# A sparse graph-attention kernel: score products with 32 weight columns per head instead of two

## The chip, the core and the metric

One NeuronCore of a Trainium2 chip runs the whole program. Its engines work side by side and wait for each other through semaphores: TensorE (matmuls, PE in the profile, with its weight loads shown as PEld), VectorE (DVE), ScalarE (ACT), GpSimd (POOL) and SyncE (SP, which here only starts DMAs). The metric is device time in microseconds of one execution. Five runs of the kernel before took 3256.15 to 3273.82 us, with a median of 3261.12 us.

## What is computed

Two graph layers over 3327 nodes with 128 features and a sparse weighted adjacency matrix. The first layer is a four-head GATv2 attention. Cut to what matters here:

```python
h = relu(layernorm(x))
for each head:
    x1, x2 = h @ w1, h @ w2
    E = leaky_relu(x1[:, None, :] + x2[None, :, :], 0.01)
    s = E @ a                          # one score for each pair of nodes
    s = exp(8 * tanh(s / 8)) * adj
    s = s / sum(s, axis=-1)
    out = leaky_relu(s @ h @ Wlin.T, 0.01)
x = x + concat(heads) @ w
```

The second layer is a graph convolution with the same matrix, relu(A_norm @ (relu(layernorm(x)) @ W.T + b)), added to x. The change touches the line `s = E @ a` of the first layer.

## The kernel before

Nodes are padded to 3328 and handled in 26 blocks of 128 rows, each in two halves of 64 rows. Only neighbours are computed: for each half, four windows of up to 8 x 128 pairs (row, neighbour) and a fifth, smaller window for what didn't fit. DVE finds the neighbours (`prep`, lines 353 to 570), POOL fetches the neighbours' rows by indirect DMA into tiles `g` (`gather`, L595), and a fixed sequence written out in `_sparse_layers` works the windows off. The order on each engine is the order in which this Python code issues instructions; `slot()` advances the older windows' tails (`finish`, `close`), the next block's preparation, and the fetches by one step each time that it is called.

A window is worked in groups. For windows 0 to 3 a group is half a window, 512 pairs; for the fifth window it is 320 pairs. `stage_z` transposes the neighbours' features on TensorE, head by head, into the PSUM tile `z` (L622; L625 and L627 for the fifth window), and DVE takes the maximum with the row's own negated features and writes `r` (L638; L633 with L635 on ACT for the fifth). With slope 0.01 the leaky part is a multiple of the plain sum, which comes from precomputed products, so that what is left of the score is one product of `r` with the vector `a` times 0.99.

`stage_r` is that product. For each of the four heads `h` it multiplies the weights `sel[:, h, ...]` with the 512 columns of `r` and writes to partitions 32h and 32h+1 of the PSUM tile `s`. `sel` holds, for each head, the vector in column 31 and zeros around it (L1139, L1140). In the kernel before it is 33 columns wide: with `at` = 0 the two columns taken are 31 and 32, with `at` = 1 they are 30 and 31, so the first half of a window lands in row 32h and the second, added to it, in row 32h+1. The rest of `s` is set to zero once (L650) and never written. The products of a window's two halves are issued together, after the second one's `r` (`k.held`): eight products in a row for windows 0 to 3 and four for the fifth, 36 for each half block.

`finish` then takes the window on: ACT copies `s` to SBUF (`ssb`, L666), TensorE transposes it (L675), DVE adds the precomputed parts to give `sc` (L678, L681), ACT computes `th` = tanh (L686) and `pe` = exp (L688), DVE multiplies with the adjacency weights into `wt` (L697), and TensorE sums the neighbours' features (L706: four column groups of 32 columns; L724 for the fifth window). `sc` and `th` come from a pool with two buffers each, so one window's may be written while the last one's is still read. A tile with one buffer has to be read out before its next writing.

When L706 is done, the window's `g` tile is free and POOL may issue the next fetch into it.

SBUF is close to full: four `g` tiles of 22,784 bytes per partition lie at the end of it.

Of the kernel before, what the change touches and what calls it, by code (L numbers as in the profile page):

```python
# [9 lines left out]
F32 = mybir.dt.float32  # L10
# [5 lines left out]
P = 128  # L16
# [215 lines left out]
def _sparse_layers(tc, nc, x, adj, w1, w2, a, wlin, w, gw, gb, gb_sb, gwT, x_sb, dinv, flag, ident, out):  # L232
# [14 lines left out]
    H = w1.shape[0]  # L247
# [5 lines left out]
    WT = 8  # L253
# [3 lines left out]
    with ExitStack() as l0:  # L257
        res = l0.enter_context(tc.tile_pool(name="res", bufs=1))
# [9 lines left out]
        w1_sb = res.tile([P, H, D], F32, name="w1_sb")  # L268
        wlinT = res.tile([P, H, D], F32, name="wlinT")
        w_sb = res.tile([P, H, D], F32, name="w_sb")  # L270
        sel = res.tile([P, H, 33], F32, name="sel")
        p_all = res.tile([P, NB, 2 * H], F32, name="p_all")
        code = res.tile([P, NP], mybir.dt.uint16, name="code")
        epos = res.tile([P, 2 * FOUND], F32, name="epos")
# [11 lines left out]
        pb = l0.enter_context(tc.tile_pool(name="pb", bufs=2))  # L286
# [358 lines left out]
        def stage_r(k, hb, m, rs):  # L645
            n = 4 * P if m < 8 else FOUND * P + HALF
            at = m % 2
            if state["scores"] is None:
                state["scores"] = ps_s.tile([P, BANK], F32, name="s")
                nc.vector.memset(state["scores"], 0.0)  # L650
            k.s = state["scores"]
            if at == 0 and m < 8:
                k.held = rs
                return
            for at, r in ((0, k.held), (1, rs)) if at else ((0, rs),):
                for h in range(H):
                    nc.tensor.matmul(k.s[32 * h:32 * h + 2, :n], sel[:, h, 31 - at:33 - at], r[h // 2][:, h % 2, :n],  # L657
                                     start=(at == 0), stop=(at == 1 or m == 8))


        def finish(k, hb, w):
            g, s = k.g.pop((hb, w)), k.s
            f0 = k.f0[hb]
            nt, nk, nm = (WT, 4, 2) if w < NW else (OVT, OVT, 1)
            ssb = ph.tile([P, BANK], F32, name="ssb", bufs=1)
            nc.scalar.copy(ssb[:, :nk * P], s[:, :nk * P])  # L666
            if w < NW:
                wq = pb.tile([P, WT, 8], F32, name="wq")
                diag = bass.AP(g.tensor, g.offset + BODY * hb, [list(g.ap[0]), [WIDE + 8, 8], [1, 8]])
                nc.vector.tensor_tensor(wq, diag, qmask[:, None, :].to_broadcast([P, WT, 8]), OP.mult)  # L670
            yield
            yield
            pt = ps_tr.tile([P, 4, P], F32, name="tr")
            for q in range(nk):
                nc.tensor.transpose(pt[:, q, :], ssb[:, q * P:(q + 1) * P], ident)  # L675
            yield
            sc = pb.tile([P, WT, H], F32, name="sc")
            nc.vector.tensor_tensor(sc[:, :nt].rearrange("p (m k) h -> p m k h", m=nm),  # L678
                                    pt.rearrange("p k (h m) -> p m k h", m=32)[:, :nm, :nk],
                                    g[:, :, f0 + D:f0 + D + H].rearrange("p (m k) h -> p m k h", m=nm), OP.add)  # L680
            nc.vector.tensor_add(sc[:, :nt], sc[:, :nt], k.pex[:, 8 * hb:8 * hb + 8] if w < NW else  # L681
                                 k.ex[:, OVT * hb:OVT * hb + OVT, 42:42 + H])
            yield
            yield
            th = pb.tile([P, WT, H], F32, name="th")
            nc.scalar.activation(th[:, :nt], sc[:, :nt], AF.Tanh, scale=1.0 / CAP)  # L686
            pe = pb.tile([P, WT, H], F32, name="pe")
            nc.scalar.activation(pe[:, :nt], th[:, :nt], AF.Exp, scale=CAP)  # L688
            yield
            yield  # L690

            if w == 0:
                k.ag = ps_a.tile([P, 2, 256], F32, name="ag")
            ag = k.ag
            if w < NW:
                wt = pv.tile([P, WT, H, 8], F32, name="wt", bufs=2)
                nc.vector.tensor_tensor(wt, pe[:, :, :, None].to_broadcast([P, WT, H, 8]),  # L697
                                        wq[:, :, None, :].to_broadcast([P, WT, H, 8]), OP.mult)
                yield
                yield  # L700
                yield
                yield
                yield
                for t in range(WT):
                    u, cg = t // 4, t % 4
                    nc.tensor.matmul(ag[32 * cg:32 * cg + 32, u, :WORK], wt[:, t].rearrange("p h q -> p (h q)"),  # L706
                                     g[:, t, f0:f0 + WORK], start=(w == 0 and t < 4), stop=False, skip_group_check=True)
                allow("g")
                return
            am = pb.tile([P, OVT, HALF], F32, name="am", bufs=1)  # L710
            wo = pv.tile([P, OVT, 8, H, 8], F32, name="wo")
            for t in range(OVT):
                nc.vector.scalar_tensor_tensor(am[:, t, :], code[:, :HALF], k.ex[:, OVT * hb + t, 41:42], g[:, t, BODY * hb:BODY * hb + HALF],
                                               op0=OP.is_equal, op1=OP.mult)
                nc.vector.tensor_tensor(wo[:, t], pe[:, t, None, :, None].to_broadcast([P, 8, H, 8]),
                                        am[:, t].rearrange("p (g q) -> p g q", q=8)[:, :, None, :].to_broadcast([P, 8, H, 8]), OP.mult)
                yield
            yield
            yield
            yield  # L720
            yield
            for t in range(OVT):
                for u in range(2):
                    nc.tensor.matmul(ag[:, u, :WORK], wo[:, t, 4 * u:4 * u + 4].rearrange("p g h q -> p (g h q)"),  # L724
                                     g[:, t, f0:f0 + WORK], start=False, stop=(t == OVT - 1), skip_group_check=True)
            allow("ge")
            tails.append(close(k, hb))
# [75 lines left out]
        for b in range(NB):  # L803
            k = Blk()
# [40 lines left out]
        def allow(kind):  # L845
            state[kind] += 1
# [345 lines left out]
        with tc.manual_schedule():  # L1192
# [4 lines left out]
            n = len(groups)  # L1197
            def scores(i):
                if 0 <= i < n:
                    b, hb, m = groups[i]  # L1200
                    stage_r(blks[b], hb, m, rs.pop(i))
                    if m % 2 or m == NG - 1:
                        ends.append(finish(blks[b], hb, m // 2))
                    slot()
# [81 lines left out]
def kernel(  # L1286
# [26 lines left out]
    gb_sb = const.tile([P, D], F32, name="gb_sb")  # L1313

    _sparse_layers(tc, nc, x, adj, w1, w2, a, wlin, w, gw, gb, gb_sb, gwT, x_sb, dinv, flag, ident, out)


# [46 lines left out]
```

## Time and profile before

| | |
|---|---|
| Median of five runs | 3261.12 us |
| Profiled execution | 3291.75 us, span 3290.0 us |
| Mean granted TensorE clock | 0.898 |
| DVE r L638, maxima | 1013.5 us busy, 832 instructions, mean 1218 ns |
| PE z L622, transposes of windows 0 to 3 | 1048.9 us busy, 6656 instructions, mean 300 ns |
| POOL g L595, indirect DMAs | 1593.1 us busy, 1664 instructions |
| ACT ssb L666, copies of s | 147.0 us busy, 260 instructions, mean 565 ns |
| ACT th L686 | 58.5 us busy, 260 instructions, mean 225 ns |
| DMA, mean over the span | 251 GB/s |

How to read it: busy time is the time in which at least one instruction of the group was running, the mean is that of one instruction, and matmuls overlap, so that count times mean is more than busy. PE rows are matmuls and PEld rows the loads of their weights. A matmul of four-byte floats is recorded as two matmuls and two loads; a transpose as one of each. In a row such as "128*2 128x512", 128*2 is rows times columns of the weights and 128x512 is the moving data. The chain of waits is followed back from the last instruction and tells where time sets the end; idle time of an engine that isn't on it costs nothing. The granted clock is the share of TensorE's clock pulses that the throttle let through.

### The profile page before, as it was taken

The page shows a single profiled execution, that of the slowest core. Times are in us where ns is not written, and L with a number is a line of the kernel's source. Part 1 is how long each engine was busy: PE and PEld are TensorE (multiplying, and loading weights), DVE is VectorE, ACT ScalarE, POOL GpSimd, SP SyncE. Part 2 cuts the span into 40 slices and gives each one's busy share as a digit, 9 for nine tenths or more (in the row PEclk, how much of TensorE's full clock was granted, in tenths as well). Part 3 has the DMA queues.
Part 4 walks back from the last instruction along what each step waited for, and adds up shares of the span by engine and source line. Part 5 has one row for each costly group of instructions (what it writes and reads, how often), then busy time and mean ns, then how long its engine had stood idle before and what let it go on. Part 6 is the DMA issues. An engine that isn't in the chain of part 4 may idle for free.

```text
span 3290.0 us, 52385 instructions
## 1 busy us (share of the span) xinstructions
PE 2564.1 (78%) x19410; PEld 1796.3 (55%) x19410; DVE 2102.2 (64%) x6426; ACT 682.1 (21%) x1703; POOL 1718.0 (52%) x1822
## 2 busy tenths in 40 slices
PE   6688777877788787778777787777877787777887
PEld 4455555555565565565555555555555555555553
DVE  6577676767667666666666665665666666665442
ACT  3122122212212221221221221221221221221110
POOL 3555555555555555545545555555555455555520
PEclk8789898998988989889989898998988999997999
DMA  9978788778877877867867867877777777777886
GB/s 320 339 263 262 242 263 276 228 260 269 265 234 257 278 215 253 275 204 261 275 211 247 266 218 242 260 246 225 260 241 230 251 256 238 245 232 224 266 265 191
DMA packets 417844, 826.94 MB, mean 251 GB/s; under 512 B 38435, under 2 KB 288815, under 8 KB 414255
## 3 DMA queue, kind: packets, MB, share of 16 engines
q0 software_dynamic: 141440, 619.41, 57.3%
q1 hardware_dynamic: 165343, 147.87, 14.5%
q10 hardware_dynamic: 110800, 56.25, 5.8%
q8 instruction: 156, 2.56, 0.3%
q14 instruction: 105, 0.86, 0.1%
HBM read 754.47 MB, written 113.22 MB: 264 GB/s over the span
## 4 chain that ended last, share of the span: by engine, by line
PE 55%; DVE 16%; issue 11%; another core or an unknown queue 9%; DMA 5%; POOL 2%; ACT 1%; SPq 0%; ACTq 0%; DVEq 0%; POOLq 0%
PE z L622 20%; PE s L657 12%; DVE r L638 9%; PE ag L706 4%; PE z L627 3%; PE tr L675 3%; DVE cand L422 2%; POOL g L595 2%; PE ag L724 2%; DMA g<-table,idx 2%; PE tr L379 2%; DVE codes L410 1%; PE tr L757 1%; PE tr L365 1%
## 5 line engine op out<-in xcount | busy, mean ns | idle before, releaser
L595 POOL DMA_INDIRECT g<-table,idx x1664 | 1593.1, 957 | 1278.7 <-PE ag L706 651.5
L638 DVE TENSOR_TENSOR r<-z,x1n 128x1024 f32<-128x1024 f32 x832 | 1013.5, 1218 | 736.2 <-remote 307.8
L622 PE MATMUL z<-ident,g 128*128 128x128 f32 x6656 | 1048.9, 300 | 216.0 <-issue 140.3
L622 PEld LDWEIGHTS z<-ident,g 128*128 128x128 f32 x6656 | 845.5, 155 | 412.0 <-issue 271.3
L657 PE MATMUL s<-r,sel 128*2 128x512 f32 (+1 forms) x3744 | 527.5, 613 | 71.7 <-issue 55.9
L666 ACT COPY ssb<-s 128x512 f32<-128x512 f32 x260 | 147.0, 565 | 854.0 <-remote 265.3
L706 PE MATMUL ag<-g,wt 128*32 128x133 f32 x3328 | 206.7, 295 | 76.7 <-issue 75.8
L657 PEld LDWEIGHTS s<-r,sel 128*2 128x2 f32 x3744 | 82.3, 85 | 336.9 <-issue 301.5
L706 PEld LDWEIGHTS ag<-g,wt 128*32 128x32 f32 x3328 | 125.1, 114 | 185.6 <-issue 176.1
L422 DVE MAX8 cand<-codes 128x8 f32<-128x52 uint16 x1664 | 217.3, 205 | 0.0
L379 PE MATMUL tr<-at,x_sb 128*128 128x128 f32 x488 | 97.5, 356 | 128.3 <-ACT at L367 102.9
L675 PE MATMUL tr<-ident,ssb 128*128 128x128 f32 x988 | 165.6, 291 | 37.2 <-ACT ssb L666 18.6
L367 ACT COPY at<-tr 128x512 f32<-128x512 f32 (+1 forms) x175 | 97.3, 556 | 393.8 <-remote 188.5
L595 POOL DMA_INDIRECT ge<-table,idxo x104 | 101.2, 973 | 145.0 <-PE ag L724 70.8
L379 PEld LDWEIGHTS tr<-at,x_sb 128*128 128x128 f32 x488 | 81.9, 251 | 153.8 <-ACT at L367 116.6
L686 ACT ACTIVATE th<-sc 128x32 f32<-128x32 f32 x260 | 58.5, 225 | 506.9 <-DVE sc L681 234.7
L675 PEld LDWEIGHTS tr<-ident,ssb 128*128 128x128 f32 x988 | 123.9, 149 | 58.8 <-ACT ssb L666 28.0
L633 DVE TENSOR_TENSOR r<-z,x1n 128x128 f32<-128x128 f32 x104 | 30.1, 290 | 185.9 <-PE z L627 120.0
L627 PE MATMUL z<-oi,x1b 128*128 128x256 f32 x416 | 131.5, 395 | 13.3 <-issue 13.2
L365 PE MATMUL tr<-ident,adjb 128*128 128x128 f32 x676 | 121.3, 307 | 25.6 <-DMA adjb<-in_adj_dram 15.5
L453 DVE MAX8 lists<-cand 128x8 f32<-128x272 f32 (+1 forms) x338 | 133.2, 394 | 2.2
L622 PE MATMUL z<-ident,ge 128*128 128x128 f32 x416 | 87.1, 285 | 42.6 <-issue 35.9
(199 smaller groups left out, 2583.8 us busy)
## 6 DMA issues: line engine op xcount, KB each, us to landing
adjb<-in_adj_dram SPq DMA_DIRECT2D x26, 1664.0 KB
table<-AT_d SPq DMA_DIRECT2D x26, 1664.0 KB
AT_d<-at ACTq DMA_DIRECT2D x150, 256.0 KB
g<-table,idx POOLq DMA_INDIRECT x1664
table<-img SPq DMA_DIRECT2D x12, 1296.0 KB
adjb<-AT_d SPq DMA_DIRECT2D x72, 128.0 KB
g<-AT_d SPq DMA_DIRECT2D x25, 256.0 KB
g<-AT_d ACTq DMA_DIRECT2D x25, 256.0 KB
```

Source lines behind the costliest of these rows:

```text
L365: nc.tensor.transpose(pt[:, q, :], adjb[:, (j0 + q) * P:(j0 + q + 1) * P], ident)
L379: nc.tensor.matmul(pq[:, :P], x_sb[:, j0 + q, :], at[:, q, :], start=(q == 0), stop=(q == js[-1]))
L422: nc.vector.max(cand[:, c, 8:].rearrange("p (r s) -> p r s", s=32)[:, :, sgm % 32], codes.rearrange("p a b -> p (a b)")[:, sgm % 32 * SEG: ...
L453: nc.vector.max(top, of)
L595: return nc.gpsimd.indirect_dma_start(out=g[:, t, lo:hi], out_offset=None, in_=tab, in_offset=bass.IndirectOffsetOnAxis(ap=at[:, t:t + 1], ...
L622: nc.tensor.matmul(z[:, i, q * P:(q + 1) * P], g[:, m % 2 * 4 + q, c0:c0 + D], ident, is_transpose=True, start=(q == 0 or m < 8), stop=(m ...
L627: nc.tensor.matmul(z[:, i, :n], k.x1b[:, h * D:(h + 1) * D], k.oi[:, hb * n:(hb + 1) * n], start=False, stop=True, skip_group_check=True)
L638: nc.vector.tensor_tensor(r.rearrange("p h (i s) -> p h i s", s=16), z.rearrange("p h (i s) -> p h i s", s=16), k.x1n[:, 2 * hp:2 * hp + 2 ...
L657: nc.tensor.matmul(k.s[32 * h:32 * h + 2, :n], sel[:, h, 31 - at:33 - at], r[h // 2][:, h % 2, :n], start=(at == 0), stop=(at == 1 or m == 8))
L666: nc.scalar.copy(ssb[:, :nk * P], s[:, :nk * P])
L675: nc.tensor.transpose(pt[:, q, :], ssb[:, q * P:(q + 1) * P], ident)
L706: nc.tensor.matmul(ag[32 * cg:32 * cg + 32, u, :WORK], wt[:, t].rearrange("p h q -> p (h q)"), g[:, t, f0:f0 + WORK], start=(w == 0 and t ...
```

## The change

`sel` becomes 63 columns wide, with the vector still in column 31. Each product takes 32 columns of it instead of two: 31 to 62 with `at` = 0 and 30 to 61 with `at` = 1. It writes all 32 partitions of its head, 30 of them with zeros (or zeros added). The number, order and moving data of the products stay. `sel` grows by 4 x 30 x 4 = 480 bytes per partition; `sc` and `th` get one buffer instead of two, which gives back 128 bytes each.

```diff
@@ -268,7 +268,7 @@
-        sel = res.tile([P, H, 33], F32, name="sel")
+        sel = res.tile([P, H, 63], F32, name="sel")
@@ -654,7 +654,7 @@
                 for h in range(H):
-                    nc.tensor.matmul(k.s[32 * h:32 * h + 2, :n], sel[:, h, 31 - at:33 - at], r[h // 2][:, h % 2, :n],
+                    nc.tensor.matmul(k.s[32 * h:32 * h + 32, :n], sel[:, h, 31 - at:63 - at], r[h // 2][:, h % 2, :n],
                                      start=(at == 0), stop=(at == 1 or m == 8))
@@ -674,7 +674,7 @@
-            sc = pb.tile([P, WT, H], F32, name="sc")
+            sc = pb.tile([P, WT, H], F32, name="sc", bufs=1)
@@ -682,7 +682,7 @@
-            th = pb.tile([P, WT, H], F32, name="th")
+            th = pb.tile([P, WT, H], F32, name="th", bufs=1)
```

## The prediction

> **What bounds the kernel now.** I read the page first: busy shares, the granted clock, the chain that ended last, and the groups of the two lines that matter here.
>
> ```profile
> PE 2564.1 (78%) x19410; PEld 1796.3 (55%) x19410; DVE 2102.2 (64%) x6426; ACT 682.1 (21%) x1703; POOL 1718.0 (52%) x1822
> PEclk8789898998988989889989898998988999997999
> ...
> PE 55%; DVE 16%; issue 11%; another core or an unknown queue 9%; DMA 5%; POOL 2%; ACT 1%; SPq 0%; ACTq 0%; DVEq 0%; POOLq 0%
> PE z L622 20%; PE s L657 12%; DVE r L638 9%; PE ag L706 4%; PE z L627 3%; PE tr L675 3%; DVE cand L422 2%; POOL g L595 2%; PE ag L724 2%; DMA g<-table,idx 2%; PE tr L379 2%; DVE codes L410 1%; PE tr L757 1%; PE tr L365 1%
> ...
> L657 PE MATMUL s<-r,sel 128*2 128x512 f32 (+1 forms) x3744 | 527.5, 613 | 71.7 <-issue 55.9
> ...
> L706 PE MATMUL ag<-g,wt 128*32 128x133 f32 x3328 | 206.7, 295 | 76.7 <-issue 75.8
> L657 PEld LDWEIGHTS s<-r,sel 128*2 128x2 f32 x3744 | 82.3, 85 | 336.9 <-issue 301.5
> L706 PEld LDWEIGHTS ag<-g,wt 128*32 128x32 f32 x3328 | 125.1, 114 | 185.6 <-issue 176.1
> ```
>
> TensorE is busiest and holds 55% of the chain; the rest is short waits shared among all engines. The score products L657 are 12% of the chain, 395 us of their 527.5 us busy, so three quarters of their time sets the end. L706 is this kernel's own example of the new form: four column groups of 32 columns at full depth, four-byte floats.
>
> Then I took both lines apart by source line (columns: count, then ns minimum/median/maximum).
>
> ```profile
> L657 PEld LDWEIGHTS s<-r,sel x3744: 80/83/129, 98.7 to 3194.7; 128*2 128x2 f32 x198
> L657 PE MATMUL s<-r,sel x3744: 431/592/1061, 98.7 to 3195.2; 128*2 128x512 f32 x176, 128*2 128x320 f32 x22
> ...
> L706 PEld LDWEIGHTS ag<-g,wt x3328: 106/110/178, 117.8 to 3205.6; 128*32 128x32 f32 x196
> L706 PE MATMUL ag<-g,wt x3328: 273/277/431, 118.3 to 3205.7; 128*32 128x133 f32 x196
> ```
>
> And a stretch of the timeline in order (start us, length us, then engine, line, count).
>
> ```profile
> 1528.84 0.11 PEld L657 LDWEIGHTS s<-r,sel 128*2 128x2 f32 x8
> ...
> 1529.27 0.10 PEld L657 LDWEIGHTS s<-r,sel 128*2 128x2 f32 x4 [0.33 <-issue]
> 1529.70 0.10 PEld L657 LDWEIGHTS s<-r,sel 128*2 128x2 f32 x4 [0.33 <-issue]
> ...
> 1530.13 0.13 PEld L706 LDWEIGHTS ag<-g,wt 128*32 128x32 f32 x4 [0.33 <-issue]
> ...
> 1530.56 0.64 PE L706 MATMUL ag<-g,wt 128*32 128x133 f32 x16
> ```
>
> Each product is recorded twice, so 26 blocks x 2 halves x 36 products are the 3744 records. The four heads run at once already: a four of loads every 0.43 us, at 1529.27, 1529.70 and 1530.13, each for the four of matmuls that follows. The last four is L706's, with 32 columns, and its matmuls start 0.43 us later too: a four of 32-column loads was hidden behind a four of streaming.
>
> **The change, part by part.** The order of instructions on every engine stays as it was; only the width of L657 and some waits differ. So nothing moves past a queue.
>
> *Streaming.* Does a 32-column product take longer than a 2-column one? L657 gives 592 ns for 512 moving columns and 431 ns for 320, so 161/192 = 0.84 ns per column. Carried down to 133 columns that is 274 ns; L706, with 32 weight columns, has 273 minimum, 277 median. The weight columns cost at most 3 ns of latency, under 2 us over 468 groups of products (26 x 2 x 9). Cost: 0.
>
> *Weight loads.* 80/83 ns becomes 106/110 ns, so 27 ns more per four (the four loads start a few ns apart and overlap). There are 3744/4 = 936 fours. If every one is covered: 0. If none is: 936 x 29 ns (the difference of the means, 114 - 85) = 27 us. In between: counting records, 1412 loads start within 4 ns of a matmul of their line, so about 353 fours stand at the head of a burst with nothing to hide behind: 353 x 27 ns = 9.5 us, of which the three quarters on the chain are 7 us. I take 7, since the timeline shows the others hidden; 0 and 27 stay as the bounds.
>
> [...] The timeline shows L657's loads at 1529.27 beside a stream that runs to 1529.70. [...]
>
> *The clock.* The granted clock is either full or half here, in steps of 3.41 us, and averages 0.898: (1 - 0.898) x 2 x 3290 = 671 us at half. If wider weights counted as more activity, this edit would buy speed. Stretches of 3.41 us (busy us and count for PE, PEld, DVE, ACT, POOL, then granted clock, DMA share, GB/s):
>
> ```profile
> 943.83:947.24 3.41, 1.30 (x7) 0.14 (x5) 2.21 (x6) 0.00 (x0) 1.90 (x2) 1.00 0.88 286
> 947.24:950.65 3.41, 3.41 (x29) 2.74 (x27) 2.54 (x11) 0.99 (x2) 1.01 (x2) 0.50 0.34 114
> ...
> 2305.74:2309.16 3.42, 1.94 (x17) 0.31 (x16) 0.44 (x4) 0.24 (x1) 2.39 (x3) 1.00 1.01 335
> 2309.16:2312.57 3.41, 3.01 (x27) 3.01 (x28) 2.23 (x10) 1.52 (x3) 0.00 (x0) 1.00 0.82 282
> ```
>
> The same stretch for L657 alone:
>
> ```profile
> 2305.74:2309.16 3.42, 1.90 (x16) 0.31 (x16) 1.00 1.01 335
> ```
>
> A stretch with 1.30 us busy is followed by half clock; one with 1.94 us, nearly all 2-column products, by full. I put this through all 762 stretches at full clock, with streaming time taken from the spacings (0.43 us per four of 512; a run of eight transposes takes 1.04 us, its last 0.27, so 0.11 us each): a streaming share under 0.37 is followed by half clock and one over it by full, with one exception. 74 stretches are over it only if the 2-column products count in full, and all 74 kept the clock. So width doesn't count. Cost: 0.
>
> *Single buffers for sc and th.* L678 must now wait until the tanh L686 has read the last sc. Among the 259 pairs in the trace the tightest is this one, from ACT's and DVE's timelines:
>
> ```profile
> 3196.44 0.23 ACT L686 ACTIVATE th<-sc 128x32 f32<-128x32 f32 x1
> 3196.70 0.23 ACT L688 ACTIVATE pe<-th 128x32 f32<-128x32 f32 x1
> ...
> 3198.65 0.17 DVE L678 TENSOR_TENSOR sc<-tr,ge 128x12 f32<-128x12 f32 x1 [8.10 <-PE tr L675]
> ```
>
> 1.97 us from the tanh's end to the next sc; the second tightest is 3.74 us. th is written and read on ACT in order, 2.12 us apart at least. Were ACT 2 us late, L678 would hold up DVE, with the maxima L638 of the next group behind it, and TensorE behind those. The built program has 162 more semaphore instructions on ACT and 8 on DVE; such records take 17 ns on ACT (median), so 2.8 us on an engine that is 79% idle. Bounds 0 and 3 us; I take 0, as ACT's own lateness is the cover.
>
> *Memory.* sel's memset grows by 120 elements once, in the start. Every tile behind sel lies 480 bytes further on, those behind sc and th 224. The maxima L422 read 32 slices 104 bytes apart, and their medians by slice are 202 to 215 ns in no order of address; gather packets of 5224 and 5248 bytes, from halves with different row starts, share a minimum of 201 ns. Nearest bounds: none to 1% of those 217 us, 2 us either way. I take 0.
>
> **Sum.** 3291.75 us is the profiled execution (span 3290.0, 1.75 around it); plus 7 is 3298.75, or +0.21%. That execution is 0.94% above the median 3261.12 and above all five runs, so I carry over the ratio: 3261.12 x 1.0021 = 3268 us.
>
> **The rivals.** (a) *Slower: the loads are paid everywhere.* Place: PEld ahead of L657. [...] Against it: L706's four fours take 0.64 us in the timeline, so they start (0.64 - 0.28)/3 = 0.12 us apart, with loads of 110 ns between. Price 27 us on 3291.75, 0.82%: 3288 us. It passes 0.5% (16.5 us) when over 570 of the 936 fours pay. (b) *Faster: width counts for the clock.* Of the 127 stretches after which the clock fell, 20 hold any score products. TensorE streams 0.75 of the half-clock time, so that time costs 671 x 0.75 / 2 = 252 us, 2.0 per fall; 20 saved are 40 us, times TensorE's 55% of the chain 22 us: 3291.75 - 22 gives 3239 us. Against it: the 74 stretches. (c) *The single buffers hold up DVE.* Each of 260 windows would have to lose 1.97 us of slack first; 3 us otherwise, 3264 us with no load term. (d) *Timing or addresses shift the falls of the clock by chance.* At 2.0 us a fall, 8 falls more or fewer are 16 us: either sign, 3245 to 3277 us. The five runs span 0.54%, so it does happen.
>
> **How the numbers follow.** Within 0.5% is about what a measurement of this kernel can tell from no change. The forecast, with (c) at 3 us in it, 0.58. (a) 0.20; (b) 0.12; (d) or a longer wait beyond 0.5%, 0.05 each way. So faster 0.12 + 0.05 = 0.17, same 0.58, slower 0.25. The range reaches from (b) to (a): 3240 to 3290. The likeliest case's own range, load term from 0 to 16 us with the runs' spread of about 8 us either way, is 3253 to 3285.
>
> **What would show it.** Loads at L657 of 106 to 110 ns; its 512-column products still 592 ns and 0.43 us apart by fours; mean clock within 0.01 of 0.898; no wait of L678 on ACT beyond the few now. I am wrong if the fours are further apart than 0.43 us at full clock, if stretches with little but L657 change which clock follows them, or if L638, L595 or a DMA changes its time per instruction, which would point to addresses.

## The result, and the profile after

The changed kernel takes 1.0021 times the kernel before, with a 95% interval of 1.001 to 1.0032 (52 runs with a median of 3281.0 us against 94 with 3274.86): 6.9 us more, 3 to 10. The forecast was +0.21% and no change by the bound of 0.5%. The number was met; what follows shows that two of the parts that it was added up from were not.

The page after, with the lines that answer to those before:

```profile
span 3298.4 us, 52555 instructions
PE 2584.2 (78%) x19410; PEld 1831.2 (56%) x19410; DVE 2100.7 (64%) x6426; ACT 683.4 (21%) x1703; POOL 1709.6 (52%) x1822
...
PE 57%; DVE 16%; issue 12%; another core or an unknown queue 8%; DMA 5%; POOL 2%; ACT 1%; ACTq 0%; SPq 0%; DVEq 0%; POOLq 0%
...
L657 PE MATMUL s<-r,sel 128*32 128x512 f32 (+1 forms) x3744 | 544.7, 619 | 89.5 <-issue 69.3
...
L657 PEld LDWEIGHTS s<-r,sel 128*32 128x32 f32 x3744 | 114.3, 113 | 340.5 <-issue 296.9
```

The loads grew by 28 ns in the mean (85 to 113), which is the row of L706 as forecast. Two single executions differ by 8.4 us of span, about what the medians of many runs differ by, but one pair proves nothing at this size: runs of one kernel on one chip spread over 50 us. Spacings in the trace, which repeat to 1 ns, tell more. TensorE's timeline of weight loads after, for a burst like the one shown of before (start us, length us, line, count):

```profile
1534.19 0.16 PEld L657 LDWEIGHTS s<-r,sel 128*32 128x32 f32 x8
1534.65 0.13 PEld L657 LDWEIGHTS s<-r,sel 128*32 128x32 f32 x4 [0.30 <-issue]
1535.08 0.13 PEld L657 LDWEIGHTS s<-r,sel 128*32 128x32 f32 x4 [0.30 <-issue]
1535.51 0.13 PEld L706 LDWEIGHTS ag<-g,wt 128*32 128x32 f32 x4 [0.30 <-issue]
```

The first four's loads are followed by the next after 0.46 us, where before it was 0.43; all later fours are 0.43 us apart as before. Counted over all such bursts at full clock, from the first four of matmuls to the second: a median of 453 ns in 174 bursts after, 429 in 172 before. So 24 ns are paid once at the head of a burst, and nothing behind it.

Why only there: going through all matmuls in order, TensorE changes 260 times from work on all 128 columns, transposes in most cases, to score products. From one transpose to the next it is 109 ns start to start; from a transpose to a score product it is 202 ns, with 2 weight columns as with 32; the 24 ns come behind that, between the first four and the second. At the change the loads aren't early: the first load starts 1 to 2 ns ahead of its matmul, at all 222 changes at full clock before and all 224 after. In the later fours, and at L706 behind L657, they are early: the loads at 1529.27 before belong to the matmuls at 1529.70 (a median of 426 ns ahead for the later products at full clock, 427 after), and use the same 128 rows as the matmuls that they run beside. What makes the change itself 93 ns longer (202 against 109) isn't shown; as it is the same with 2 and with 32 columns, it is no part of the difference.

### The profile page after: what moved, and what is told of

Same layout as the page of the kernel before. It is cut to its first block, busy times and chain, and to the rows that moved or that the text cites. A ratio compares the mean times of both kernels' runs of the same rounds, so it can differ in the third digit from the quotient of the medians.

```text
span 3298.4 us, 52555 instructions
## 1 busy us (share of the span) xinstructions
PE 2584.2 (78%) x19410; PEld 1831.2 (56%) x19410; DVE 2100.7 (64%) x6426; ACT 683.4 (21%) x1703; POOL 1709.6 (52%) x1822
## 4 chain that ended last, share of the span: by engine, by line
PE 57%; DVE 16%; issue 12%; another core or an unknown queue 8%; DMA 5%; POOL 2%; ACT 1%; ACTq 0%; SPq 0%; DVEq 0%; POOLq 0%
PE z L622 21%; PE s L657 12%; DVE r L638 9%; PE ag L706 4%; PE z L627 3%; PE tr L675 3%; DVE cand L422 2%; PE tr L379 2%; PE ag L724 2%; POOL g L595 2%; DMA g<-AT_d 1%; DVE codes L410 1%; PE tr L365 1%; DMA g<-table,idx 1%
## 5 line engine op out<-in xcount | busy, mean ns | idle before, releaser
L638 DVE TENSOR_TENSOR r<-z,x1n 128x1024 f32<-128x1024 f32 x832 | 1013.1, 1218 | 776.2 <-PE z L622 316.5
L657 PE MATMUL s<-r,sel 128*32 128x512 f32 (+1 forms) x3744 | 544.7, 619 | 89.5 <-issue 69.3
L657 PEld LDWEIGHTS s<-r,sel 128*32 128x32 f32 x3744 | 114.3, 113 | 340.5 <-issue 296.9
L706 PE MATMUL ag<-g,wt 128*32 128x133 f32 x3328 | 224.5, 298 | 96.6 <-issue 95.9
L706 PEld LDWEIGHTS ag<-g,wt 128*32 128x32 f32 x3328 | 131.4, 115 | 209.4 <-issue 198.8
L365 PE MATMUL tr<-ident,adjb 128*128 128x128 f32 x676 | 121.1, 306 | 26.3 <-DMA adjb<-in_adj_dram 16.8
L456 DVE MATCH_REPLACE8 cand<-lists,cand 128x272 f32<-128x272 f32 (+1 forms) x312 | 118.1, 378 | 0.0
```

The lines of the kernel that those rows point to most:

```text
L365: nc.tensor.transpose(pt[:, q, :], adjb[:, (j0 + q) * P:(j0 + q + 1) * P], ident)
L638: nc.vector.tensor_tensor(r.rearrange("p h (i s) -> p h i s", s=16), z.rearrange("p h (i s) -> p h i s", s=16), k.x1n[:, 2 * hp:2 * hp + 2 ...
L657: nc.tensor.matmul(k.s[32 * h:32 * h + 32, :n], sel[:, h, 31 - at:63 - at], r[h // 2][:, h % 2, :n], start=(at == 0), stop=(at == 1 or m = ...
```

## The experiments

All times are ratios to the kernel before in runs on the same chip. The twelve runs fell on three chips, on which the kernel before takes 3408, 3278 and 2501 us; only ratios within one chip are compared.

### Widening alone, and memory alone

`wide33` takes 32 columns without more room: with the vector in column 1, columns 1 to 32 and 0 to 31 do the same as the changed kernel's.

```diff
-                nc.vector.tensor_scalar(sel[:, :, 31], aT, 1.0 - SLOPE, None, op0=OP.mult)
+                nc.vector.tensor_scalar(sel[:, :, 1], aT, 1.0 - SLOPE, None, op0=OP.mult)
-                    nc.tensor.matmul(k.s[32 * h:32 * h + 2, :n], sel[:, h, 31 - at:33 - at], ...
+                    nc.tensor.matmul(k.s[32 * h:32 * h + 32, :n], sel[:, h, 1 - at:33 - at], ...
```

> The products take 32 weight columns out of a 33-column sel with the vector moved to column 1, so that no tile changes size, address or number of buffers. Theory (the longer load is paid once at each change from transposes to column-tiled products, 260 times): loads of 105 to 110 ns, 453 ns instead of 429 between the first four and the second of a burst, later fours still 429 apart; time +0.10% to +0.30% on the kernel before. Rival, memory (single buffers or moved addresses cost it): within 0.05% of the kernel before. Rival, all fours pay: +0.8%.

`narrow63` is the changed kernel with the old product line, so its memory alone:

```diff
-                    nc.tensor.matmul(k.s[32 * h:32 * h + 32, :n], sel[:, h, 31 - at:63 - at], ...
+                    nc.tensor.matmul(k.s[32 * h:32 * h + 2, :n], sel[:, h, 31 - at:33 - at], ...
```

> The changed kernel's memory (63 columns of sel, one buffer for sc and th, all addresses as there) with two-column products. Theory: 429 ns between first and second four, time within 0.1% of the kernel before. Rival, memory: +0.1% to +0.3% here, as much as the whole change.

Measured, on the chip with 3408 us: `wide33` 1.0010 (0.9987 to 1.0033), with 453 ns at the head of a burst (median of 180) as expected; `narrow63` 1.0038 (1.0016 to 1.006), with 429 ns. The theory was right about the head and failed on the time: two-column products with the changed memory were slower by more than the changed kernel is over all its runs, and widening alone could not be told from nothing. Both were run once more:

> The changed kernel's memory with two-column products, once more, beside other runs of the kernel before. If the memory costs 0.2% to 0.4% wherever it runs, that again; if the first look owed it to its chip or to chance, within 0.15%.

> 32 columns without any change of memory, once more. Theory: +0.1% to +0.25% (260 x 24 ns = 6.2 us, 0.19%, less what lies off the chain).

On the chip with 2501 us: `narrow63_again` 1.0031 (1.0019 to 1.0042), `wide33_again` 1.0001 (0.9988 to 1.0013). On both chips, then, the changed memory (addresses and single buffers together) costs 0.3 to 0.4%, and widening nothing that can be told from zero. The 260 heads x 24 ns are 6.2 us, 0.25% of 2501; the second interval of `wide33` ends at 0.13%, or 3.3 us, so on that chip about half of them or more lies off the chain. On the first chip the interval of `wide33` reaches to 0.33%, and all 6.2 us would still fit in it.

### Values and width

`filled63` is the changed kernel with the vector in the 30 spare columns too, except the two beside it, so rows of `s` are filled that `sc` doesn't read:

```diff
+                nc.vector.tensor_scalar(sel[:, :, 33:], aT[:, :, None].to_broadcast([P, H, 30]), 1.0 - SLOPE, None, op0=OP.mult)
                 nc.vector.tensor_scalar(sel[:, :, 31], aT, 1.0 - SLOPE, None, op0=OP.mult)
```

> The changed kernel with the 30 spare columns holding the score vector instead of zeros (two columns next to it stay zero); the rows of s that this fills are read by no later step's result. Theory: a load and a product cost by columns, not by values, so the same as the changed kernel, +0.1% to +0.3% on the kernel before, 453 ns at the head of a burst, mean granted clock 0.89 to 0.91. Rival, zeros spare the clock: clock lower by over 0.01 and time over +0.5%.

> 16 weight columns of a 33-column sel, vector in column 1, nothing else changed. Theory (what a load lasts beyond some 80 ns is paid at the head of a burst, by its length): loads of about 92 to 96 ns, 440 ns (436 to 444) between first and second four, time 0 to +0.2%. Rival, a fixed cost of using more than a few columns: 453 ns, as with 32 columns.

`wide16` has 16 columns (rows 32h to 32h+15, columns 1 - at to 16 - at). Measured: `filled63` 1.0047 (1.0026 to 1.0069), 453 ns at the head, mean clock 0.885 where the four profiles of this chip have 0.885 to 0.887. There is no sign that zeros spare the clock. The time is above the 0.1% to 0.3% that I had expected: the ratio is `narrow63`'s 1.0038 plus `wide33`'s 1.0010. `wide16` 1.0000 (0.9979 to 1.0021) and a head of 440 ns (median of 186). Its loads by source line (columns as before):

```profile
L657 PEld LDWEIGHTS s<-r,sel x3744: 92/96/151, 98.4 to 3326.8; 128*16 128x16 f32 x198
```

Loads of 80, 92 and 105 ns (minimum) give heads of 429, 440 and 453: 12 and 25 ns more of load are 11 and 24 ns more at the head, nearly one for one.

### The head's cost, six times over

To see the 24 ns in the time itself, the eight products of a window were spread: each is issued behind a transpose of the next group's second pair of heads instead of all together. `spread2` does it with two columns, `spread32` with `wide33`'s 32; no tile moves.

```diff
                     for q in range(n // P):
                         nc.tensor.matmul(z[:, i, q * P:(q + 1) * P], g[:, m % 2 * 4 + q, c0:c0 + D], ident,
                                          is_transpose=True, start=(q == 0 or m < 8), stop=(m < 8), skip_group_check=True)
+                        if hp == 1 and state["todo"]:
+                            state["todo"].popleft()()
...
-                    nc.tensor.matmul(k.s[...], sel[...], r[h // 2][:, h % 2, :n],
-                                     start=(at == 0), stop=(at == 1 or m == 8))
+                    state["todo"].append(partial(nc.tensor.matmul, k.s[...], sel[...], r[h // 2][:, h % 2, :n],
+                                                 start=(at == 0), stop=(at == 1 or m == 8)))
```

> Two-column products, but each of a window's eight put behind its own transpose instead of all eight together, so that 1664 of the 1872 products stand alone behind a change from transposes to column-tiled work. Much slower than the kernel before, as four heads no longer run at once (about 1872 x 0.86 us against 468 x 0.86 us: some 1000 us more). It is the base for the next run.

> The same with 32 columns out of a 33-column sel, no tile moved. Theory (24 ns are paid at each change into column-tiled work): over 1664 heads more than the run with two columns by 25 to 45 us (1664 x 24 ns = 40, less what lies off the chain), 6 times the whole change. Rival, the load costs nothing and memory makes the difference: 0 to 8 us. Rival, each load is paid, 3744 x 27 ns: 100 us.

Measured, on the chip with 2501 us: 3740.21 us (3739.93 to 3740.98) and 3783.02 us (3779.76 to 3784.24), 42.8 us apart. The first is 1240 us above the kernel before, where I had expected some 1000. The groups of TensorE in `spread2` and then in `spread32` (busy us, mean ns; the products now stand at the line that issues them):

```profile
L625 PE MATMUL s<-r,sel 128*2 128x512 f32 (+1 forms) x3320 | 1629.9, 573 | 0.0
L622 PE MATMUL z<-ident,g 128*128 128x128 f32 x6656 | 1189.4, 287 | 97.9 <-DVE r L640 72.7 <-DVE dv L791 18.8 <-DMA g<-table,idx 3.0
```

```profile
L625 PE MATMUL s<-r,sel 128*32 128x512 f32 (+1 forms) x3320 | 1671.5, 585 | 0.0
L622 PE MATMUL z<-ident,g 128*128 128x128 f32 x6656 | 1189.5, 287 | 96.8 <-DVE r L640 72.4 <-DVE dv L791 18.8 <-DMA g<-table,idx 2.6
```

The products' busy time grows by 41.6 us and the transposes' by 0.1. There are 1789 visits to score products (I had expected 1664), 1712 of them straight from work on all 128 columns, and at full clock they have 428 and 453 ns: 1712 to 1789 x 24.5 ns = 42 to 44 us. TensorE is busy for 94% here, so nearly all of it reaches the end. This shows the cost of a head and its size, and that loads behind a head are free: all 3744 loads at 27 ns would be 101 us, and they aren't there.

### What in the memory

Three runs take the changed memory apart, on the chip with 3278 us. `single33` has one buffer for `sc` and `th` and a filler of 256 bytes behind them, so that only `th` moves; `pad224` and `pad192` have a gap behind `sel` and nothing else.

```diff
# single33
-            sc = pb.tile([P, WT, H], F32, name="sc")
+            sc = pb.tile([P, WT, H], F32, name="sc", bufs=1)
-            th = pb.tile([P, WT, H], F32, name="th")
+            th = pb.tile([P, WT, H], F32, name="th", bufs=1)
+            if state["gap"]:
+                pb.tile([P, 2 * WT, H], F32, name="gap", bufs=1)
+                state["gap"] = False
# pad224 (pad192: 48)
         sel = res.tile([P, H, 33], F32, name="sel")
+        res.tile([P, 56], F32, name="gap")
```

> One buffer each for sc and th and nothing else: two-column products out of 33 columns, and a filler that leaves every other tile at its address. Theory now (widening costs about 0.1%, the rest of the changed kernel's time comes from its memory): if the single buffers do it, +0.2% to +0.4% on the kernel before; if the addresses do it, within 0.15%.

> The kernel before with a gap of 224 bytes behind sel, so that the four g tiles, r and all tiles behind sel start at 32 instead of 0 from a multiple of 64 (the g tiles at exactly the changed kernel's addresses); two columns, two buffers. If the addresses do it, +0.2% to +0.4%; if the single buffers do it, within 0.15%.

> The same with a gap of 192 bytes, so that the g tiles still start at multiples of 64 but no longer of 256. If addresses matter by 64 bytes: within 0.15% of the kernel before, unlike the gap of 224. If they matter by 256 bytes: +0.2% to +0.4% here too. If the single buffers do it: both gaps within 0.15%.

> The changed kernel once more beside these. Theory: the sum of widening (+0.1%) and of whichever of the three others is slower, +0.2% to +0.5%.

Measured: `single33` 1.0008 (0.9975 to 1.0041), `pad224` 0.9995 (0.9965 to 1.0026), `pad192` 1.0020 (0.9992 to 1.0048), the changed kernel 1.0024 (1.0000 to 1.0047). On this chip an interval is 0.3% to either side, too wide to part them: inconclusive in time.

The traces part them in another way. Of the packets of 512 bytes, counted by their duration, this share takes exactly 27 ns, with the mean in ns beside it (queue 1 is SP's, queue 10 ACT's; 144,132 and 105,984 such packets):

```
                        queue 1          queue 10
before                  79.0%  29.29     83.0%  27.61
single33                78.4%  29.40     82.0%  27.67
wide33 (3408 us chip)   77.9%  29.39     82.5%  27.66
after                   70.1%  29.77     58.1%  28.03
changed_again           71.3%  29.89     60.7%  28.06
pad224                  71.4%  29.85     61.3%  28.07
pad192                  69.8%  30.01     57.3%  27.78
narrow63 (3408 us chip) 69.4%  29.95     55.1%  28.20
wide33_again (2501 us)  89.1%  28.28     98.7%  27.26
narrow63_again (2501)   78.8%  28.94     86.7%  28.04
```

On one chip and in one order of work, whatever moves the tiles behind `sel` is in one class, and whatever leaves them is in the other; the single buffers don't matter to it. (In the other order, `spread2` has 59% on queue 1 with no tile moved.) But a share over the whole run says neither where the packets change nor which way: on queue 10 most of the lost share went to less than 27 ns, so to shorter packets (23% after, 3% before). Split in time, the picture is clear. The last stretch begins when the first strip of the matrix for the second layer is fetched into a `g` tile (L898, `g<-AT_d`, on both queues) and lasts to the end. Mean of the packets of 512 bytes of both queues in it and ahead of it, and how long it lasts:

```
                         in the last stretch   ahead of it   the stretch lasts
before                        27.7 ns            28.8 ns         122.7 us
single33                      27.8               28.8            125.2
wide33 (3408 us chip)         27.8               28.8            122.6
wide16 (3408)                 27.9               28.8            122.7
wide33_again (2501)           27.9               27.9            123.1
after                         31.6               28.5            127.6
changed_again                 31.6               28.6            127.8
pad224                        31.7               28.5            127.6
pad192                        31.6               28.5            126.4
narrow63 (3408)               31.9               28.6            127.8
filled63 (3408)               32.1               28.7            126.5
narrow63_again (2501)         31.7               27.9            129.2
```

So the slower packets are those of the last stretch, 4 ns more for each of some 44,000, and ahead of it these packets are no slower. `pad224` and `pad192` have nothing but the move, so the move does it. The stretch is longer in all seven traces with moved tiles (126.4 to 129.2 us) than in all seven without (122.6 to 125.7; `spread2` and `spread32` have 125.1 and 125.7), by 4.5 us between the medians. On the chip with 3278 us the one trace without, `single33`, leaves only 1 to 3 us. How the packets reach the time there is seen in the chain of waits: `g<-AT_d` holds 26.3% of the last stretch before and 35.7% after.

In the built programs the `g` tiles start at multiples of 256 bytes before, 224 bytes past them after, and 192 past them in `pad192`. So with starts at multiples of 64 alone, as `pad192` has them, the packets of the last stretch still take 31.6 ns against 27.7; 128 was not tried, and by what means the start makes a packet longer isn't shown. The shorter packets of queue 10 belong to another transfer: `AT_d<-at` reads the tile `at`, which starts 128 bytes past a multiple of 256 before, 96 after and 64 in `pad192`, and about a quarter of its packets took 26 ns after and 25 ns in `pad192`. On the chip with 2501 us they stayed at 27.

That chip is also where DMA is busiest: its share is 0.98 from 200 to 2300 us in `narrow63_again`, against 0.77 from 200 to 3000 us in the profile of the kernel before. The queues there, first of `wide33_again`, then of `narrow63_again` (packets, MB, share of 16 engines):

```profile
span 2492.9 us, 52385 instructions
q0 software_dynamic: 141440, 619.41, 70.7%
q1 hardware_dynamic: 165343, 147.87, 18.5%
q10 hardware_dynamic: 110800, 56.25, 7.5%
```

```profile
span 2510.1 us, 52555 instructions
q0 software_dynamic: 141440, 619.41, 70.4%
q1 hardware_dynamic: 165343, 147.87, 18.6%
q10 hardware_dynamic: 110800, 56.25, 7.7%
```

The same bytes, yet more time: the packets' durations add up to 16 x 2425.4 and 16 x 2441.6 us, 16.2 us per engine more, of which queue 1 has 6.1, queue 10 5.4 and queue 0 4.6. Of the 11.5 us of queues 1 and 10, 10.9 lie in the last stretch; where the share is 0.98, their packets of 512 bytes take 27.9 ns in both. Queue 0's part says nothing: `wide33` and `wide16`, neither moved, differ by 8.5 us there. The last stretch is 6.1 us longer in this pair, and the runs' medians differ by 7.6. So moved addresses slow the packets of the last stretch, on all three chips, and the stretch grows with them. That this is all that the memory costs isn't shown, and no kernel with the addresses alone was slower as a whole beyond its interval.

## Why the prediction was right, and where it wasn't

**The load term** was forecast with 9.5 us of TensorE time and 7 on the chain. The duration was right (+27 ns forecast, 25 to 28 measured), the place was right (heads only), and the count too high: I counted 1412 early loads as 353 fours, but whole visits are 260, each paying 24 ns: 6.2 us. The share on the chain was the weak link. Three quarters came from L657's part of one chain of waits, but `wide33` has +0.10% and +0.01%, and on the second chip at most about half of 6.2 us. Time that stands on the chain of one execution isn't time that can be added one for one. What takes up such a delay, no run shows.

**The memory term** was forecast as nothing: "I take 0". That step failed. Its bound of 2 us came from DVE's maxima, and of DMA it weighed only the gather packets of two sizes at 201 ns. (That is their median and not, as I wrote, their minimum, which is 199; both stayed the same.) It left out the 512-byte packets of the two other queues, which take 4 ns more in the last stretch, and the stretch some 4.5 us. The prediction's own sign of being wrong, a DMA that changes its time and so points to addresses, did come. The two runs with the changed memory and two columns put the whole term at 0.38% and 0.31%. So the number was met by luck, as far as these runs tell: a term that was too large stood in for one that was left out.

**Streaming** at no cost: right. 592 ns for 512 columns with 2, 16 and 32 weight columns, and 429 ns between later fours.

**The clock** at no cost: right. In the trace after, 67 stretches of 3.41 us exceed a streaming share of 0.37 only through the score products, and 66 kept full clock; before it was 74 of 74. Rival (b) falls, and `filled63` takes away its twin, that zeros spare the clock: 0.885, where the four profiles of that chip have 0.885 to 0.887.

**Single buffers** at no cost: the tightest pair is 2.03 us apart after, 1.97 before, and the 162 further semaphore records on ACT have a median of 17 ns as estimated. `single33` doesn't show more than 0.4%, and can't show less.

**Rival (a)**, every load paid: excluded by the later fours at 429 ns and by 42.8 instead of 100 us between the spread kernels.

Open: how the changed kernel's 6.9 us divide. The last stretch has 4.9 of them in the two profiles (127.6 against 122.7 us), the heads at most 6.2, and single buffers below 0.4% aren't excluded. I did not run the 63-column `sel` with every later tile at its old address.

## What to carry to other kernels

Here wider weight loads took more of TensorE's time, 24 ns at each, only at the 260 changes to score products, where they didn't start ahead of their matmuls, and none in the later fours, which stayed 429 ns apart; so count such changes in the trace, not the loads, and see whether TensorE is the bound there. When a tile grows, the tiles behind it move, here the `g` tiles by 224 bytes: look at where DMA targets then start (in the last stretch packets took 27.7 to 27.9 ns with `g` tiles at multiples of 256 bytes, and 31.6 to 32.1 with starts 192 or 224 bytes past one), and compare packet durations by their mean and stretch by stretch, not by a minimum or over the whole run: here they cost time where the DMA was waited for, in the last 4 to 5% of the kernel, and not where it was busiest. If a longer mask is wanted, first see whether the one that is there can be read from another column, as `wide33` did without a byte more.

## What the runs showed that I had not expected

The same kernel before takes 2500.75, 3278.22 and 3408.37 us (medians) on three chips. Single instructions last alike (L638 1218 ns in the kernel before's profile, 1214 in `wide33_again`); the DMA share, 0.77 there and 0.98 in `narrow63_again`, doesn't. What makes the slower chips slower was not followed up.

In these traces streaming time alone told what TensorE's clock would do: in five profiles of 762 to 770 stretches each at full clock, a share under 0.37 of 3.41 us foretold half clock for the next one and a share over it full clock, with 1 to 9 exceptions, whether products had 2, 32 or 128 weight columns, and transposes counted like any matmul.
